# An adaLN attention and feed-forward block on one Trainium2 core: the gate's columns made earlier, a load of x made later, b2's rows behind b1's

## The chip, the core and the metric

The kernel runs on one core of a Trainium2 chip. The metric is the device time of one execution in microseconds; lower is better. In the profile, PE is TensorE (matmuls), PEld its weight loads, DVE VectorE, ACT ScalarE, POOL GpSimd and SP the engine that issues most of the DMAs. "SPq" and "ACTq" are the sequencers of SP and ACT when they issue a DMA.

## What is computed

There are 8 batches of 1024 rows of 256 numbers, all in f32. Each batch has six vectors of 256 that come from its condition `c`; two of them are gates, kept away from zero.

```
mod = (silu(c) @ wmod).reshape(8, 6, 1, 256)          # sa, ca, ga, sb, cb, gb
ga, gb = sign(g) * max(|g|, 0.25)                      # for both gates
h = layernorm(x) * (1 + ca) + sa
x = x + ga * softmax((h*w_lhs) @ (h*w_rhs).T) @ h
h = layernorm(x) * (1 + cb) + sb
x = x + gb * (relu(h @ W1 + b1) @ W2 + b2)             # W1 256x1024, W2 1024x256
```

## The kernel before

**Tiles and steps.** A batch is worked in eight steps of 128 rows (`i`, 0 to 7) and kept as two halves of 512 rows (`x_t[b, g]`). The main loop runs over batches and steps. Step `i` of batch `b` makes the scores of a row block two steps ahead (`direct`, matmuls at L433; steps 6 and 7 make those of the next batch's rows 0 and 1), takes their row maximum (`row_max`, L484), turns the maximum on PE (`max_turn`, L489), subtracts (`subtract`, L496), applies the exponent on ACT (`exponent`, L505) and multiplies by the normalized x (`product`, L522 and the paired forms). From batch 1 on, the feed-forward of the batch before is spread over the same steps: `pair_products` (L730, PSUM tiles pa, pb, pc), `pair_sums`, `pair_last`, `pair_relu`, and the second matrix (L810). Batch 0 has no feed-forward beside it.

**Mirrored scores.** The score matrix is symmetric up to the two weight vectors, so only blocks on and right of the diagonal are multiplied. `mirror(b, i)` fills the rest. In batch 0 it does so with transposes on PE. From batch 1 on, DVE turns 32 x 32 blocks (L456, tile Tm), four DMAs on SP write them to a scratch in DRAM (L327, `D_m<-Tm`), and a fifth reads them back in their new place (L330, `sc<-D_m`). The maximum of row `i` needs the mirrored blocks of all rows above it. The same five DMAs (`move`) turn the normalized x of the next batch (`D_a`; for batch 1 it is read back into `Y_early` and `X_early`, in steps 2 and 3 of batch 0, and used by `prepare_turn` in steps 5 and 6, which makes lT and rT, L386 and L396) and the input of the feed-forward (`D_f`, read back to X_f and used by `ffn_turn`, L709 and L711).

**What sets the order.** The order of the program's lines is kept on each engine (`pin`), so an instruction that waits holds all behind it on its engine; SP's DMAs are issued in order too. Loads of x for the next batches go out on ACT's queue (`load_x`, L86), into six buffers.

**The columns.** Four small row tiles are loaded at the start, turned on PE and copied by ACT into `cols` (`columns`, L178 and L179): `wv` holds w_lhs, w_rhs and b2 as six rows of 128, `b1_rows` holds b1 as eight. `w_cols(side)` picks two columns: side 0 is w_lhs, 1 is w_rhs, 2 is b2. `wv` is turned early in the start, `b1_rows` in `make_columns`, in step 0 of batch 0.

**The gate of the feed-forward.** `mod_direct` (L225) makes the feed-forward's vectors as columns, in the start. `make_gcol` makes the gate from them (four DVE instructions, L992 to L995), multiplies it by b2 (L1034), and stores for the last batch both results in DRAM (`last_d`, two DMAs at L1036 on SP, 256 numbers each, one by one since neighbours in a row of `gcol` are a batch apart). `gcol` is read from step 4 of batch 1 on (`y_gate`, L861, at 126.6 us) and `last_d` near the end (L899, at 696.2 us). `make_gcol` is called by `keep_columns`, in step 6 of batch 0, between the transpose of the scores of batch 1's row 0 and their maximum.

**The start.** SP issues in this order: c, x (second quarter of batch 0), w_lhs, w_rhs, b2, the last two quarters of x, the last two thirds of wmod (L119), b1 (L120), W1, W2 and the x of batch 1. ACT's queue takes the first quarter of x and the first third of wmod. PE waits at 12.07 us for wmod's later part (`mod_rows(2, 1)`, L198).

Of the kernel before, what the change touches and what calls it, by code (L numbers as in the profile page):

```python
# [13 lines left out]
ALU = mybir.AluOpType  # L14
# [3 lines left out]
P = 128  # L18
# [6 lines left out]
def adaln_block_kernel(  # L25
# [13 lines left out]
    nc = tc.nc  # L39
# [3 lines left out]
    ND = D // P  # L43
    NI = INTER // P
# [39 lines left out]
    def load_x(b, g, queue=nc.scalar):  # L84
        x_t[b, g] = two.tile([P, TH, D], F32, tag="x", name=f"x_{b}_{g}", bufs=6)
        queue.dma_start(  # L86
            out=x_t[b, g],
            in_=x[b, ts(g, HALF), :].rearrange("(t p) d -> p t d", p=P),
        )
# [3 lines left out]

    early_d = two.tile([P, 4, D], F32, tag="X", name="early_d", bufs=1)
    c_sb = early_d[:B, 0]
    wv, b1_rows = early_d[: 3 * ND, 2, 0:P], early_d[:NI, 3, 0:P]
    nc.sync.dma_start(out=c_sb, in_=c)
    for g in range(2):
        x_t[0, g] = two.tile([P, TH, D], F32, tag="x", name=f"x_0_{g}", bufs=6)
# [2 lines left out]
    def load_x0(q, queue):  # L102
        queue.dma_start(out=x_t[0, q // 2][:, ts(q % 2, 2), :], in_=x0_v[:, ts(q, 2), :])
# [9 lines left out]
    nc.sync.dma_start(  # L113
        out=wv[ND : 2 * ND, :], in_=w_rhs.rearrange("a b (k p) -> (a b k) p", p=P)
    )
    nc.sync.dma_start(out=wv[2 * ND : 3 * ND, :], in_=b2.rearrange("(k p) -> k p", p=P))
    load_x0(2, nc.sync)
    load_x0(3, nc.sync)
    nc.sync.dma_start(out=wm[:, :, 2 * D : 6 * D], in_=wmod_v[:, :, 2 * D : 6 * D])  # L119
    nc.sync.dma_start(out=b1_rows, in_=b1.rearrange("(k p) -> k p", p=P))  # L120
    w1 = const.tile([P, ND, INTER], F32, name="w1")
    w2 = const.tile([P, NI, D], F32, name="w2")
    nc.sync.dma_start(out=w1, in_=W1.rearrange("(k p) i -> p k i", p=P))
# [49 lines left out]
    cols = const.tile([P, NI + 3 * ND], F32, name="cols")  # L173

    def columns(src, at):
        n = src.shape[0]
        pv = ps_t.tile([P, HALF], F32, tag="t", name=f"pt_v{at}")
        nc.tensor.transpose(pv[:, :n], src, ident[:n, :n])  # L178
        nc.scalar.copy(cols[:, ds(at, n)], pv[:, :n])  # L179

    b1_col = lambda i: cols[:, i : i + 1]

    w_cols = lambda side: cols[:, ds(NI + side * ND, ND)].rearrange(
        "p (k b) -> p k b", b=1
    ).to_broadcast([P, ND, B])

# [6 lines left out]
    def mod_rows(part, parts):  # L193

        pm = ps_a.tile([P, HALF], F32, tag="a", name=f"pmr_{part}")
        w = parts * D
        for k in range(ND):
            nc.tensor.matmul(  # L198
                pm[:B, :w],
                lhsT=scT[:, k, :],  # L200
                rhs=wm[:, k, ds(part * D, w)],
                start=(k == 0),
                stop=(k == ND - 1),
            )
        nc.scalar.copy(
            mod[:, part : part + parts, :].rearrange("b s d -> b (s d)"), pm[:B, :w]
        )
# [73 lines left out]
    def prepare_stats(b, g, tiles=range(TH)):  # L281

        if tiles[0] == 0:
            mv = work.tile([P, TH, 2], F32, tag="mva", name=f"mva_{b}_{g}")
            pre[b, g] = [mv]
        mv = pre[b, g][0]
        for j in tiles:
            stats(mv, j, x_t[b, g][:, j, :], f"a{b}_{g}_{j}")

    def prepare_rstd(b, g):  # L290
        pre[b, g].append(rstd_of(pre[b, g][0], "ra", f"ra_{b}_{g}"))

    def prepare_norm(b, g, tiles=range(TH)):

        mv, r = pre[b, g]
        if b > 0:
            shift = work.tile([P, TH], F32, tag="rs", name=f"rs_{b}_{g}")
            nc.vector.scalar_tensor_tensor(shift, mv[:, :, 0], -1.0, r, ALU.mult, ALU.mult)
        for j in tiles:
            t = g * TH + j  # L300
            if b > 0:
                nc.scalar.activation(
                    xg_t[b][:, t, 0:D], x_tile(b, t), AF.Identity,
                    scale=r[:, j : j + 1], bias=shift[:, j : j + 1],
                )
                continue
            engine = nc.vector if j < TH // 2 else nc.gpsimd
            engine.tensor_scalar(
                xg_t[b][:, t, 0:D], x_tile(b, t), mv[:, j, 0:1], r[:, j : j + 1],
                ALU.subtract, ALU.mult,  # L310
            )
# [346 lines left out]
    def spare():  # L658
        if queue:
            queue.popleft()()  # L660
# [4 lines left out]
    def ffn_rstd(b, g):  # L665
        mv = mvb_t.pop((b, g))
        ffn["r", g] = mv, rstd_of(mv, "rb", f"rb_{b}_{g}")
# [15 lines left out]
    def x_plus(b, g):  # L683

        for t in range(g * TH, (g + 1) * TH):
            xr = x_tile(b, t)
            later(xr, xr, rows_t[b][:, 1, :], ALU.add)

    def xg_times(b, g):

        for t in range(g * TH, (g + 1) * TH):
            xg = xg_t[b][:, t, 0:D]
            later(xg, xg, rows_t[b][:, 0, :], ALU.mult)
# [256 lines left out]
    prepare_stats(0, 0, range(2, TH))  # L950
    prepare_rstd(0, 0)
    mod_rows(0, 2)
    columns(wv, NI)
    prepare_stats(0, 1, range(2))
    prepare_norm(0, 0)
    prepare_stats(0, 1, range(2, TH))
# [33 lines left out]
    def make_gate(out, raw, size, sign):  # L990

        nc.vector.tensor_scalar(sign, raw, 0.0, 2.0, ALU.is_ge, ALU.mult)  # L992
        nc.vector.scalar_tensor_tensor(size, raw, -1.0, raw, ALU.mult, ALU.max)
        nc.vector.tensor_scalar(size, size, GATE_MIN, None, ALU.max)
        nc.vector.scalar_tensor_tensor(out, sign, -1.0, size, ALU.add, ALU.mult)  # L995
# [33 lines left out]
    gcol = const.tile([P, 2, ND, B], F32, name="gcol")  # L1029
    last_d = dram.tile([2, D], F32, name="last_d")  # L1030

    def make_gcol():
        make_gate(gcol[:, 0], mod_ffn[:, 2], MB[:, 0], MB[:, 1])
        nc.vector.tensor_tensor(gcol[:, 1], gcol[:, 0], w_cols(2), ALU.mult)  # L1034
        for j in range(2):
            nc.sync.dma_start(  # L1036
                out=last_d[j].rearrange("(k p) -> p k", p=P), in_=gcol[:, j, :, B - 1]
            )
# [33 lines left out]
    def make_columns():  # L1072
        columns(b1_rows, 0)
        nc.gpsimd.tensor_tensor(b1_step, cols[:, NH:NI], cols[:, 0:NH], ALU.subtract)

    def keep_columns():
        nc.vector.tensor_copy(modT[:, 0], mod_ffn[:, 0])
        nc.vector.tensor_scalar(modT[:, 1], mod_ffn[:, 1], 1.0, None, ALU.add)
        make_gcol()

    def early(b, i):

        if b == 0:

            if i in (1, 2):
                prepare_rstd(1, i - 1)
            elif i == 4:
                ffn_rstd(0, 0)
            if i in (1, 2):
                prepare_norm(1, i - 1)  # L1090
                x_plus(1, i - 1)
            if i in (3, 4):
                xg_times(1, i - 3)
            elif i == 5:
                prepare_turn(1, 0)
                ffn_norm(0, 0)
            elif i == 6:
                load_x(2, 0)
        else:
            if i == 2 and b + 1 < B:  # L1100
                prepare_norm(b + 1, 0)
            elif i == 6 and b + 2 < B:
                load_x(b + 2, 0)
# [24 lines left out]
    def norms(b, i):  # L1128
        if b > 0 and i == 0:
            ffn_blocks(b - 1, 1)  # L1130
        if b == 0:
            if i == 0:
                prepare_start(1)
        elif b + 1 < B:
            if i == 1:
                prepare_start(b + 1)
                prepare_stats(b + 1, 0)
            elif i == 2:
                prepare_blocks(b + 1, 0)
                x_plus(b + 1, 0)  # L1140
                xg_times(b + 1, 0)
        elif i == 5:

            ffn_blocks(b, 0)
        if b == B - 1:
            return
        if i == 6 and b > 0:
            ffn_blocks(b, 0)
# [7 lines left out]
    for b in range(B):  # L1156
        for i in range(NT):
# [27 lines left out]
            if b == 0:  # L1185
                if ahead[0] == 0:
                    row_max(*ahead)
                else:
                    mirror(*ahead)
                turns(b, i)  # L1190
                product(b, i, (0,))
                spare()
                if i in (0, 1):
                    prepare_stats(1, i)
                if ahead[0] == 0:
                    mirror(*ahead)
                if last_exponent:
                    exponent(*last_exponent)
                last_exponent = ahead if ahead[0] == 0 else None
                early(b, i)  # L1200
                spare()
                product(b, i, (1,))
                if ahead[0] == 0:
                    max_turn(*ahead)
                product_out(b, i)
                spare()
                if ahead[0] == 0:
                    subtract(*ahead)
                if i == 0:
                    make_columns()  # L1210
                norms(b, i)
                spare()
                if i == NT - 1:
                    assert not queue
                    right_sums(1, range(4))
                continue
# [243 lines left out]
```

## Time and profile before

| | us |
|---|---|
| median of 3 runs | 768.96 |
| lowest and highest run | 765.62, 770.04 |
| the profiled execution | 765.82 |
| its span, first to last instruction | 764.0 |
| PE busy in it | 750.9 |
| busy DVE, POOL, ACT | 572.2, 571.0, 376.4 |

The span's mean granted TensorE clock is 0.998 of full speed. The times in the views count from the span's start; the profiled execution takes 1.82 us more than its span. "Idle before" and the arrow behind an instruction name what its engine waited for last.

Where things stand in time around the change: step 1 of batch 0 ends on PE at 38.8 us, step 6 runs from 58.1 and step 7 from 68.0; batch 1 begins at 71.7.

### The profile page before, as it was taken

How to read it: one execution, taken by the hardware profiler on the slowest of the kernel's cores; microseconds unless marked ns; L12 is line 12 of the kernel's file. 1: busy time of each engine (PE TensorE's matmuls, PEld its weight loads, DVE VectorE, ACT ScalarE, POOL GpSimd, SP SyncE). 2: the span in 40 equal slices, each digit the busy share in tenths (PEclk: the TensorE clock that was granted, in tenths of full speed). 3: DMA queues.
4: the chain of work that ended last, by engine and by line, in shares of the span. 5: the costliest groups of instructions: out<-in, count | busy, mean ns of one | idle time of the engine just before them, and what ended most of it. 6: DMA issues, size and time to landing. Idle time of an engine off the chain costs nothing.

```text
span 764.0 us, 11903 instructions
## 1 busy us (share of the span) xinstructions
PE 750.9 (98%) x3876; PEld 625.1 (82%) x3876; DVE 572.2 (75%) x1261; ACT 376.4 (49%) x690; POOL 571.0 (75%) x658
## 2 busy tenths in 40 slices
PE   8999799999999999999999999999999999999998
PEld 3786588888898888978888888888889788888887
DVE  6786588868787786968779688886879677685632
ACT  3465444644466353754537454464546635243521
POOL 3761677679978789687886889777996788669731
PEclk9999999999999999999999999999999999999999
DMA  8033743355534554435534455335552454133220
GB/s 302 17 112 112 104 137 98 116 154 157 153 96 124 169 170 125 113 120 164 152 107 145 127 154 159 95 115 154 159 165 66 130 167 140 50 89 127 79 88 28
DMA packets 107466, 96.24 MB, mean 126 GB/s; under 512 B 30318, under 2 KB 99972, under 8 KB 107404
## 3 DMA queue, kind: packets, MB, share of 16 engines
q1 hardware_dynamic: 99660, 86.84, 39.7%
q10 hardware_dynamic: 7744, 8.65, 3.6%
q8 instruction: 30, 0.49, 0.3%
q14 instruction: 32, 0.26, 0.1%
HBM read 51.13 MB, written 44.32 MB: 125 GB/s over the span
## 4 chain that ended last, share of the span: by engine, by line
PE 90%; DMA 4%; DVE 3%; ACT 1%; issue 1%; SPq 1%; DVEq 0%
PE psc L433 16%; PE pa L730 10%; PE po L522 9%; PE pr L614 7%; PE pb L730 6%; PE yc L810 6%; PE pc L730 6%; PE ya L810 6%; PE yb L810 6%; PE pq L614 5%; PE pp L570 5%; PE py L920 4%; PE yd L810 3%; DMA D_m<-Tm 1%; DMA wm<-in_L_wmod_dram 1%; PE pm L489 1%
## 5 line engine op out<-in xcount | busy, mean ns | idle before, releaser
L433 PE MATMUL psc<-rT,lT 128*128 128x512 f32 (+3 forms) x384 | 135.0, 487 | 0.5 <-ACT rT L363 0.5
L784 POOL TENSOR_TENSOR f<-f,kept 128x512 f32<-128x512 f32 x64 | 81.5, 1274 | 49.7 <-DVE f L783 23.0
L505 ACT ACTIVATE pT<-pT 128x1024 f32<-128x1024 f32 x64 | 67.6, 1056 | 75.4 <-DVE pT L496 75.3
L440 ACT COPY sc<-psc 128x512 f32<-128x512 f32 (+3 forms) x96 | 44.8, 475 | 114.4 <-PE psc L433 106.2
L496 DVE TENSOR_TENSOR pT<-sc,pm 128x1024 f32<-128x1024 f32 x64 | 77.3, 1208 | 30.2 <-PE pm L489 14.9
L433 PEld LDWEIGHTS psc<-rT,lT 128*128 128x128 f32 x384 | 66.4, 191 | 38.0 <-issue 25.5
L484 DVE TENSOR_REDUCE m<-sc 128x1 f32<-128x1024 f32 x64 | 77.4, 1209 | 11.2 <-DMA sc<-D_m 9.1
L522 PE MATMUL po<-xg,pT 128*128 128x257 f32 x352 | 80.7, 380 | 0.5 <-DVE rs_f L675 0.5
L522 PEld LDWEIGHTS po<-xg,pT 128*128 128x128 f32 x352 | 66.2, 190 | 11.3 <-issue 1.2
L751 ACT COPY kept<-pa 128x512 f32<-128x512 f32 x64 | 37.4, 584 | 71.2 <-PE pa L730 71.2
L730 PE MATMUL pb<-hs,w1s 128*128 128x256 f32 x256 | 66.7, 383 | 1.8 <-DVE f L769 1.1
L730 PE MATMUL pc<-hT,w 128*128 128x256 f32 x256 | 65.7, 379 | 0.0
L884 POOL TENSOR_TENSOR x<-x,Y 128x512 f32<-128x512 f32 x28 | 35.1, 1277 | 30.8 <-DMA Y<-D_y 25.4
L730 PEld LDWEIGHTS pb<-hs,w1s 128*128 128x128 f32 x256 | 49.0, 192 | 9.7 <-DVE f L769 2.0
L793 ACT ACTIVATE f<-f 128x512 f32<-128x512 f32 x64 | 39.8, 623 | 33.8 <-POOL f L784 33.7
L663 POOL TENSOR_TENSOR x<-x,rows 128x256 f32<-128x256 f32 x64 | 44.8, 732 | 13.7 <-ACT rows L1025 10.5
L730 PEld LDWEIGHTS pc<-hT,w 128*128 128x128 f32 x256 | 48.7, 190 | 6.7
L810 PE MATMUL yc<-f,w2s 128*128 128x256 f32 x224 | 51.3, 379 | 0.0
L456 DVE STREAM_TRANSPOSE Tm<-sc 128x896 f32<-128x896 f32 (+6 forms) x49 | 34.3, 700 | 19.0 <-ACT sc L440 17.0
L810 PEld LDWEIGHTS yc<-f,w2s 128*128 128x128 f32 x224 | 41.5, 190 | 8.1 <-issue 2.9
L570 PEld LDWEIGHTS pp<-xg,pT 128*128 128x128 f32 x336 | 41.9, 192 | 5.1 <-issue 1.4
L803 POOL TENSOR_TENSOR ft<-f 128x256 f32<-128x256 f32 x56 | 40.8, 729 | 6.5 <-ACT f L794 6.5
(164 smaller groups left out, 1820.1 us busy)
## 6 DMA issues: line engine op xcount, KB each, us to landing
D_f<-T_f SPq DMA_DIRECT2D x64, 128.0 KB, 2.4
X_f<-D_f SPq DMA_DIRECT2D x16, 512.0 KB, 3.5
D_a<-T_a SPq DMA_DIRECT2D x56, 128.0 KB, 2.3
D_y<-T_y SPq DMA_DIRECT2D x56, 128.0 KB, 2.7
Y<-D_y SPq DMA_DIRECT2D x14, 512.0 KB, 4.7
out_dram<-x SPq DMA_DIRECT2D x14, 512.0 KB, 4.4
x<-in_L_attn_x_dram ACTq DMA_DIRECT2D x12, 512.0 KB, 3.3
X_a<-D_a SPq DMA_DIRECT2D x12, 512.0 KB, 3.5
```

The lines of the kernel that those rows point to most:

```text
L433: nc.tensor.matmul(psc[:, : hi - lo], lhsT=lT_t[b, i // TH][:, k, ts(i % TH, P)], rhs=rT_t[b, n][:, k, lo - n * HALF : HALF], start=(k == ...
L440: nc.scalar.copy(score_row(b, i)[:, lo // V : hi // V, :], psc[:, : hi - lo].rearrange("p (n v) -> p n v", v=V),)
L484: nc.vector.tensor_reduce(m, score_row(b, i), AX.XY, ALU.max)
L496: nc.vector.tensor_tensor(pT.rearrange("p j (a v) -> p j a v", v=V), score_columns(b, i), pm[:, :P].rearrange("p (j a v) -> p j a v", j=1, ...
L505: nc.scalar.activation(pT_t[b, i], pT_t[b, i], AF.Exp)
L522: nc.tensor.matmul(po[:, : D + 1], lhsT=pT[:, t, :], rhs=xg_t[b][:, t, 0 : D + 1], start=(t == 0), stop=(t == NT - 1),)
L570: nc.tensor.matmul(out, lhsT=lhs[:, t, :], rhs=xg_t[b][:, h * TH + t, P : P + XS], start=(t == 0), stop=(t == TH - 1),)
L614: nc.tensor.matmul(out, lhsT=lhs[:, t, :], rhs=rhs[:, t, :], start=(t == 0), stop=(t == TH - 1),)
L663: queue.append(lambda: nc.gpsimd.tensor_tensor(out, in0, row, op))
L730: nc.tensor.matmul(out, lhsT=lhsT, rhs=rhs, start=True, stop=True)
L784: nc.gpsimd.tensor_tensor(f[:, c::NH, hi], f[:, c::NH, hi], kept[:, None, hi].to_broadcast([P, 2, H2]), ALU.add,)
L810: nc.tensor.matmul(out, lhsT=lhs(c), rhs=rhs(c), start=(c == 0), stop=(c == NH - 1))
```

## The change

`make_gcol` moves from `keep_columns` (step 6 of batch 0) to step 1 of batch 0, behind that step's `subtract`, with its five DVE instructions and its two stores. The load of the first half of x of batch 2 moves from step 6 to step 7 of batch 0; there it stands on ACT behind the second instruction of `ffn_turn`. The load of b2 moves on SP from the third of the small row loads to behind b1, and its rows are turned together with b1's in `make_columns` instead of with w_lhs and w_rhs; so `wv` has four rows in place of six, `b1_rows` ten in place of eight, and the order of `cols` is b1, b2, w_lhs, w_rhs. `make_gcol` can so not stand ahead of `make_columns` (step 0).

```diff
-    wv, b1_rows = early_d[: 3 * ND, 2, 0:P], early_d[:NI, 3, 0:P]
+    wv, b1_rows = early_d[: 2 * ND, 2, 0:P], early_d[: NI + ND, 3, 0:P]
...
-    nc.sync.dma_start(out=wv[2 * ND : 3 * ND, :], in_=b2.rearrange("(k p) -> k p", p=P))
     load_x0(2, nc.sync)
     load_x0(3, nc.sync)
     nc.sync.dma_start(out=wm[:, :, 2 * D : 6 * D], in_=wmod_v[:, :, 2 * D : 6 * D])
-    nc.sync.dma_start(out=b1_rows, in_=b1.rearrange("(k p) -> k p", p=P))
+    nc.sync.dma_start(out=b1_rows[0:NI], in_=b1.rearrange("(k p) -> k p", p=P))
+    nc.sync.dma_start(out=b1_rows[NI:], in_=b2.rearrange("(k p) -> k p", p=P))
...
-    w_cols = lambda side: cols[:, ds(NI + side * ND, ND)].rearrange(
+    w_cols = lambda side: cols[:, ds(NI + ND + side * ND, ND)].rearrange(
...
-    columns(wv, NI)
+    columns(wv, NI + ND)
...
     def make_gcol():
         make_gate(gcol[:, 0], mod_ffn[:, 2], MB[:, 0], MB[:, 1])
-        nc.vector.tensor_tensor(gcol[:, 1], gcol[:, 0], w_cols(2), ALU.mult)
+        nc.vector.tensor_tensor(gcol[:, 1], gcol[:, 0], w_cols(-1), ALU.mult)
         for j in range(2):
             nc.sync.dma_start(
                 out=last_d[j].rearrange("(k p) -> p k", p=P), in_=gcol[:, j, :, B - 1]
             )
...
     def keep_columns():
         nc.vector.tensor_copy(modT[:, 0], mod_ffn[:, 0])
         nc.vector.tensor_scalar(modT[:, 1], mod_ffn[:, 1], 1.0, None, ALU.add)
-        make_gcol()
...
-            elif i == 6:
+            elif i == 7:
                 load_x(2, 0)
...
                 if i == 0:
                     make_columns()
+                elif i == 1:
+                    make_gcol()
                 norms(b, i)
```

## The prediction, made before the result was known

> **What bounds the kernel now.** I read the page's busy shares, then the waits of the PE (TensorE) queue, then busy time by stretch, and then the chain and the order of time for the one stretch that stands out.
>
> ```profile
> PE 750.9 (98%) x3876; PEld 625.1 (82%) x3876; DVE 572.2 (75%) x1261; ACT 376.4 (49%) x690; POOL 571.0 (75%) x658
> ```
>
> The waits (engine and line, what it waited for: us in all, times, longest):
>
> ```profile
> PE pa L730 <- ACT kept L751: 3.0, 1, 3.0
> ...
> PE pb L730 <- DVE f L769: 1.1, 1, 1.1
> PE pm L489 <- DVE m L484: 0.6, 1, 0.6
> PE pb L730 <- POOL hs L720: 0.6, 1, 0.6
> ```
>
> PE is busy 98% of 764.0 us, so some 13 us are open in all, and the few waits above are nearly all of what is open in mid-kernel. They lie in one place (columns: stretch, its length, busy PE, PEld, DVE, ACT, POOL, granted clock, DMA share, GB/s):
>
> ```profile
> 60.00:74.00 14.00, 14.00 (x49) 8.99 (x48) 9.48 (x23) 6.65 (x12) 0.47 (x1) 1.00 0.49 145
> 74.00:100.00 26.00, 20.21 (x80) 15.22 (x79) 16.24 (x33) 10.65 (x21) 16.75 (x19) 0.93 0.67 104
> 100.00:190.00 90.00, 89.97 (x478) 75.79 (x477) 71.83 (x158) 47.23 (x87) 73.28 (x84) 1.00 0.45 132
> ```
>
> From 74 to 100 us, where batch 0 hands over to batch 1, PE is open for 5.79 us and its granted clock falls to 0.93; behind it PE is full for 90 us, and so it is to about 590. What PE gains at 100 us therefore reaches the end. The chain through that stretch (start, length):
>
> ```profile
> 75.03 0.60 SPq L1036
> ...
> 77.65 9.17 DMA D_m<-Tm
> ...
> 86.90 4.08 DMA sc<-D_m
> ...
> 95.62 2.64 PE pa L730 x6
> ```
>
> D_m, the mirrored scores of row 1 of batch 1, needs 9.17 us to land; its kind (96 KB) has a median of 3.3. Ahead of it on SP's queue stand the two `last_d` stores of L1036. After it comes everything in order: the read back to sc, row 2's maximum on DVE at 91.00, the subtraction of row 1 at 92.14, the exponent on ACT, behind which `kept` waits in ACT's order, and PE's pa at 95.62. The DMA view of 76 to 78 us shows what the stores are:
>
> ```profile
> DMA packets 1170, 0.53 MB, mean 264 GB/s; under 512 B 565, under 2 KB 1170, under 8 KB 1170
> ```
>
> Two stores of 1 KB with 4 bytes at a time make 512 of these 565 small packets. From 80 to 85 us next to nothing moves (3 to 7 GB/s; 8 packets from 80 to 82) though D_m has not landed; at about 85.6 its packets go on. I read this as D_m held by the stores until 10.6 us after their first issue.
>
> Before that, X_f of batch 0 is late, beside the 512 KB load of x for batch 2:
>
> ```profile
> 65.24 0.38 ACTq L86 DMA_DIRECT2D x<-in_L_attn_x_dram  x1
> ...
> 72.90 0.55 DVE L709 TENSOR_SCALAR hT<-X_f,modT 128x512 f32<-128x512 f32 x1 [3.01 <-DMA X_f<-D_f]
> ...
> 77.95 1.22 DVE L484 TENSOR_REDUCE m<-sc 128x1 f32<-128x1024 f32 x1 [3.15 <-DMA sc<-D_m]
> ```
>
> **The change, part by part.** *make_gcol leaves keep_columns.* Five DVE instructions of 0.17 us (67.00 to 67.87, 0.87 us together) and the stores' 1.12 us of issue leave step 6 of batch 0. On DVE nothing follows: the next two, a maximum of 1.21 and the transpose at 68.92, wait there for a score copy that ends at 68.82. On SP the stores leave the way of D_m(1,1). Without them I let it land in 3.3 us. Its issue starts right behind the read of sc(1,0): in before 74.37, so landing would be near 80, the read's 4.08 gives 84, and DVE, which has finished L783 at 85.09, would go straight on to row 2's maximum instead of at 91.00. Then the subtraction, the exponent and `kept` are done before PE asks. What goes: PE's open time from 90 to 96 (0.33 + 1.68 + 1.62 = 3.63 us by stretches of 2 us), and the clock. Behind the 3.02 us wait the granted clock reads 0.50 at 96:98 and 0.66 at 98:100: six pa need 2.64 us (1.30 at 127.95, at full clock), four pb 1.47 (0.86). That is 1.34 + 0.61 = 1.95 us. Together **5.58 us**.
>
> The Trainium skill, "TensorE: Matmul & The Clock Gate" (Part 1), lets the clock fall to half after about one idle window of 3.4 us and says that this window runs free; the row (3.02 us open, then 0.50) fits, and by that rule the 1.95 us would differ from run to run, so that the sum below would be anything from 4.8 to 6.7 us.
>
> *x of batch 2 a step later.* In step 7, ACT issues the load behind L711, which waits for X_f, so at about 71 to 72 instead of 65.24. X_f then shares the engines no longer. A quiet D_f lands 1.85 us behind its last issue (719.69 to 721.54; here 65.19 to 67.48, 2.29), X_a needs 3.5 (here 67.48 to 72.86, 5.4): X_f is there up to 2.3 us earlier, at 70.6. The wait of pb for POOL's hs (0.56) goes. D_m(1,0), 4.6 us from last issue to the read in before, lands at 72 to 73 and its read to sc starts 1.4 to 2.5 us earlier. But there the x load now lies: 512 KB at 357 or 264 GB/s (stretches 6:7 and 76:78) are 1.5 to 2.0 us, of which I charge 0.8 to 1.3 to that read. Sc(1,0) is in place 0.6 to 1.9 us earlier, and so are the chain of DVE behind it (77.95), the pb wait of 1.13 us and the exponent that product(1,0) waits for at 83.21 (0.47 us). Ends 0.6 and 1.9 us with the delay of the next part in them; I take **1.2**, the middle. The later load costs nothing by itself: its statistics are first read at 102.94.
>
> *make_gcol arrives in step 1.* DVE takes its 0.87 us behind L496 (ends 41.79). The row maxima that follow end 0.4, 0.4 and 0.1 us before PE turns them (44.33, 49.42, 53.97), and DVE's open times at 44.37 (0.3 us) and 53.36 (0.8) take the rest: nothing, at most 0.3. The stores go out at 42.7 on an empty queue, and behind them on SP stands the following (start, issue time, engine, line):
>
> ```profile
> 44.40 1.79 SPq L327 DMA_DIRECT2D D_a<-T_a  x4
> 48.14 0.34 SPq L330 DMA_DIRECT2D Y_early<-D_a  x1
> 49.81 2.83 SPq L327 DMA_DIRECT2D D_a<-T_a  x4
> 54.57 0.34 SPq L330 DMA_DIRECT2D X_early<-D_a  x1
> ```
>
> D_a is what they can hold now. From below, nothing: Y_early is read at 48.9, later only by DVE's delay. From above, as D_m was held: it landed 11.8 us after the first store's issue, so the read is at 54.5. I take 54.0, near the upper end, as that row is the only one of these stores; the sc read that stood ahead of them in before is missing. Then Y_early lands at 57.5 (3.5 as X_a), in time for 57.72. The second D_a (1.95 to issue, as at 165.65, and 2.6 to land) lets X_early be read at 58.9, in place at 62.4. ACT's two rT (1.50) end at 63.9; PE asks at 63.3 for the second half of direct(1,0). So PE loses 0.6 us, already in the 0.6 to 1.9 above; every us beyond a read at 53.4 costs one. The Trainium skill, "DMA: Bandwidth & Descriptors" (Queues, rings and completion order), says that a completion signal lands only after every earlier write of that DMA engine. By this D_a inherits the stores' whole delay; that is the upper end, and speaks against the change.
>
> *b2 behind b1.* One issue of 0.25 us leaves SP ahead of load_x0(2), and one of 0.30 arrives behind wmod, ahead of W1, which starts at 6.03 with a wait for the first wmod half and is needed at 28.79. wmod's second half, for which PE waits 1.20 us at 12.07, is issued at 4.12 and may go out 0.3 to 0.6 earlier. But the DMA share is 1.0 from 3 to 16 us, all loads ahead of it stay ahead, and so I book nothing (0 to 0.6 gained). The column copies keep their count; 6 become 4 columns, 8 become 10.
>
> **Sum.** 5.58 + 1.2 = 6.8, less 0.1 for DVE: 6.7 us. The profiled execution took 765.82 (span 764.0 and 1.8 around it): 759.1. It is one of the fast ones of runs from 765.62 to 770.04; 6.7 off their median is 762.3. Outside this stretch PE waits for nothing over 0.5 us between 100 and 700, so part of the spread may lie in it; the profile can't say. I take **760.5**, between the two, and 757 to 764.5 as this case's own range.
>
> **Rivals.**
> *The late sc(1,1) stays late* (0.15): what held D_m was not the stores, or the x load, now queued ahead of it, takes their place. For it: the load is 512 KB at just that time. Against it: the other six D_m of this size land in 3.3, and DMA is nearly idle from 80 to 85. The 5.58 us stay and 1.1 go: 764.7, by the median 767.9.
> *D_a held too long* (0.06), slower: the stores hold D_a longer than they held D_m, as 512 packets of D_a join them. Each us after 53.4 delays X_early, rT and direct(1,0); from 3 us of wait on, the clock adds its 1.95. It outweighs the gain from a read at about 59, and with a read at 64 (21 us after the stores' issue) the time is 759.1 + 10 + 1.95 = 771. For it: 9.17 us was already far from 3.3. Against it: those packets were gone 10.6 us after issue with a busier queue.
> *The start gains too* (0.07): wmod's second half lands earlier by what SP waits less, PE's 1.20 us go: 758, by the median 761.
> *The forecast* (0.72).
>
> A measurement can tell 0.5%, 3.8 us, from no change: faster is under 765.1. The forecast and the start's gain are faster, 0.79; the late sc is within, 0.15; the held D_a is slower, 0.06. To leave out no more than 2 in 10 the range runs from 756.5 to 767.9, the late sc included.
>
> **What would show it.** Right: D_m(1,1) lands in 3 to 4 us; the granted clock is 1.00 from 74 to 100; no 3.0 us wait of pa for `kept`; the read of Y_early moves from 48.14 to about 54; an rT wait of some 0.6 us at 63. Wrong: Y_early still read at 49 (the stores are cheap on an empty queue: step priced too high), a D_m behind the x load that still lands after 9 us, or a wait over 3 us at 61 to 66.

## The result and the profile after

The changed kernel takes 763.43 us (median of 12 runs, 760.78 to 766.28) against 767.43 us (12 runs, 764.06 to 770.04): 4.0 us less, ratio 0.9949 with a 95% interval of 0.9928 to 0.9970. The forecast was 760.5 us, a gain of 6.7. It had the direction, and the place where time is won; in the profile, more than half of what is won there is given back elsewhere. The profiled execution took 764.15 us, span 762.4; it is to be compared with the 765.82 of before with care, since the 12 executions of either kernel spread over 5 us and more, and only one of each has a trace.

First the stretches, with the same columns as in the prediction:

```profile
44.00:60.00 16.00, 15.61 (x75) 12.69 (x74) 14.57 (x27) 8.86 (x18) 8.57 (x13) 1.00 0.38 54
60.00:74.00 14.00, 11.71 (x34) 6.71 (x33) 9.16 (x21) 7.54 (x13) 0.00 (x0) 0.88 0.44 138
74.00:100.00 26.00, 25.53 (x115) 20.27 (x114) 19.19 (x38) 12.76 (x23) 17.26 (x19) 1.00 0.56 170
```

From 74 to 100 us PE is open for 0.47 us where it was 5.79, at a clock of 1.00 where it was 0.93: the stall of the hand-over is gone. But from 60 to 74, where PE had been full, it is now open for 2.29 us and the clock is 0.88. SP's own rows say why (start, length of the issue):

```profile
44.55 0.88 SPq L1036 DMA_DIRECT2D last_d<-gcol  x2
47.09 8.93 SPq L327 DMA_DIRECT2D D_a<-T_a  x4
57.78 0.34 SPq L330 DMA_DIRECT2D Y_early<-D_a  x1
58.22 1.91 SPq L327 DMA_DIRECT2D D_a<-T_a  x4
63.18 0.34 SPq L330 DMA_DIRECT2D X_early<-D_a  x1
...
78.21 2.14 SPq L327 DMA_DIRECT2D D_m<-Tm  x4
83.50 0.52 SPq L330 DMA_DIRECT2D sc<-D_m  x1
```

The lower two rows are the forecast's gain: D_m(1,1) is read back 3.15 us behind its last issue, no longer 8.8. The upper five are the price: D_a stands behind the two stores now. Its four issues, 1.79 us in before, take 8.93, its read waits until 57.78, and X_early's read moves from 54.57 to 63.18. That ends on PE (two rows of the changed kernel, in order of time):

```profile
66.42 1.52 ACT L396 ACTIVATE rT<-X_early,sides 128x512 f32<-128x512 f32 x2 [1.25 <-DMA X_early<-D_a]
...
68.00 6.68 PE L433 MATMUL psc<-rT,lT 128*128 128x512 f32 x12 [2.29 <-ACT rT L396]
```

ACT makes rT only when X_early is there, and PE stands still for 2.29 us. The clock then reads 0.84, 0.50 and 0.80 in the three stretches of 2 us from 68. The same twelve matmuls of the scores (PSUM tile psc), behind the same wait but at a clock of 1.00, need 4.99 us in the run with make_gcol alone (below):

```profile
66.59 4.99 PE L433 MATMUL psc<-rT,lT 128*128 128x512 f32 x12 [1.89 <-ACT rT L396]
```

One ledger for the two profiled executions, in us of PE's time:

| place | lost before | lost after | won |
|---|---|---|---|
| start, to the first matmul of L225 (begins at 25.42, after at 25.16) | | | 0.3 |
| fall of the clock at 28 us (see the last section) | 0 | 1.7 | -1.7 |
| 44 to 74 us | 0 | 0.39 and 2.29 open, 1.7 by the clock (6.68 less 4.99) | -4.4 |
| hand-over, 74 to 100 us | 5.79 open, 1.95 by the clock | 0.47 open | 7.3 |

Together 1.5 us are won by this count; the spans differ by 1.6.

### The profile page after: what moved, and what is told of

It is laid out like the page before. It is cut to its first block, busy times and chain, and to the rows that moved or that the text cites. A ratio compares the mean times of both kernels' runs of the same rounds, so it can differ in the third digit from the quotient of the medians.

```text
span 762.4 us, 11902 instructions
## 1 busy us (share of the span) xinstructions
PE 752.6 (99%) x3876; PEld 625.8 (82%) x3876; DVE 574.5 (75%) x1261; ACT 376.5 (49%) x690; POOL 570.9 (75%) x658
## 4 chain that ended last, share of the span: by engine, by line
PE 92%; DVE 3%; DMA 2%; ACT 1%; SPq 1%; issue 1%; DVEq 0%; ACTq 0%
PE psc L433 15%; PE pa L730 10%; PE pr L614 7%; PE po L522 7%; PE pc L730 7%; PE pb L730 7%; PE yc L810 6%; PE ya L810 6%; PE yb L810 6%; PE pq L614 5%; PE pp L570 5%; PE py L920 4%; PE yd L810 3%; PE pm L489 1%; SPq L327 1%; DMA D_a<-T_a 1%
## 5 line engine op out<-in xcount | busy, mean ns | idle before, releaser
L433 PE MATMUL psc<-rT,lT 128*128 128x512 f32 (+3 forms) x384 | 136.9, 492 | 2.9 <-ACT rT L396 2.9
L522 PE MATMUL po<-xg,pT 128*128 128x257 f32 x352 | 81.9, 384 | 0.5 <-DVE rs_f L675 0.5
L522 PEld LDWEIGHTS po<-xg,pT 128*128 128x128 f32 x352 | 67.0, 192 | 11.5 <-issue 1.2
L751 ACT COPY kept<-pa 128x512 f32<-128x512 f32 x64 | 37.4, 584 | 69.4 <-PE pa L730 67.2
L718 POOL TENSOR_TENSOR hs<-hT 128x256 f32<-128x256 f32 x16 | 11.6, 726 | 46.1 <-DVE hT L709 46.1
L570 PEld LDWEIGHTS pp<-xg,pT 128*128 128x128 f32 x336 | 41.9, 192 | 5.1 <-DVE st_b L262 1.4
```

Source lines behind the costliest of these rows:

```text
L433: nc.tensor.matmul(psc[:, : hi - lo], lhsT=lT_t[b, i // TH][:, k, ts(i % TH, P)], rhs=rT_t[b, n][:, k, lo - n * HALF : HALF], start=(k == ...
L522: nc.tensor.matmul(po[:, : D + 1], lhsT=pT[:, t, :], rhs=xg_t[b][:, t, 0 : D + 1], start=(t == 0), stop=(t == NT - 1),)
L570: nc.tensor.matmul(out, lhsT=lhs[:, t, :], rhs=xg_t[b][:, h * TH + t, P : P + XS], start=(t == 0), stop=(t == TH - 1),)
```

## The experiments

The theory after the result: the two stores of 4-byte pieces hold all DMA work queued behind them for some 12 us, wherever they stand; the change moved the hold from D_m to D_a and made it cheaper, not free. (The hold is counted here from the first store's issue to the read of the DMAs queued behind it.) The first rival: the gain comes from the x load.

**The three parts alone.** Each is the kernel before with one part of the diff.

> One part alone: make_gcol with its two stores in step 1; the x load stays in step 6, b2 stays where it was. Theory (the two stores of 4-byte pieces hold whatever DMA writes are queued behind them for some 10 us; the change moved that hold from D_m to D_a): D_m(1,1) lands in 3 to 4 us, the 3.0 us wait of pa for kept and the half clock at 96 to 100 are gone, the read of Y_early moves from 48 to about 54 to 58, an rT wait of 1 to 2.5 us appears at 61 to 68; 2 to 4 us faster than before. Rival (the gain comes from the x load leaving the way of D_f, X_f and D_m): within 1 us of before, the D_m beside the x load still late.

> One part alone: the x load of batch 2 in step 7; the stores stay in step 6, in front of D_m(1,1). Theory: D_m(1,1) still takes 9 us or more to land and the wait for kept with its half clock stays; X_f lands 1 to 2 us earlier; 0 to 1.5 us faster than before. Rival (the x load was the cause): 3 to 4 us faster, D_m(1,1) lands in under 5 us.

> One part alone: b2's rows behind b1's. Theory: wmod's second half is issued about 0.5 us earlier and lands a few tenths earlier; within 0.5 us of before. Rival (the half clock seen near 28 us in the changed kernel comes from the earlier start): the granted clock falls at 28 to 32 here too, and the time is 1 to 2 us longer than before.

The edits are lines of the diff above, in the second only this one:

```diff
-            elif i == 6:
+            elif i == 7:
                 load_x(2, 0)
```

| | median us | ratio to before | 95% interval |
|---|---|---|---|
| before, of these runs (31) | 766.21 | | |
| make_gcol alone (12) | 764.71 | 0.9991 | 0.9967 to 1.0014 |
| x load alone (12) | 762.87 | 0.9962 | 0.9941 to 0.9983 |
| b2 alone (12) | 765.59 | 0.9998 | 0.9975 to 1.0021 |

The ratio is not the quotient of the two medians beside it: for make_gcol alone that would be 0.9980, which lies in the interval. The three ratios multiplied make 0.9951, the whole 0.9949. How they divide was not expected: make_gcol alone gains 0.7 us by its ratio (the interval goes from 2.5 gained to 1.1 lost), where 2 to 4 were expected, as its rival had it. Its trace is as the theory had it: D_m(1,1) is read 2.4 us behind its last issue, the hold has moved as in the changed kernel, and the rT wait is 1.9 us:

```profile
43.53 0.88 SPq L1036 DMA_DIRECT2D last_d<-gcol  x2
46.08 7.68 SPq L327 DMA_DIRECT2D D_a<-T_a  x4
56.49 0.34 SPq L330 DMA_DIRECT2D Y_early<-D_a  x1
```

The time from the turn of b1's rows in step 0 (L178) to the first matmul of L570 in batch 1 (tile pp) spans the places that the change touches and leaves out the start and the fall of the clock at 28. It is 68.5 us in before, 65.3 here and 67.2 with the x load alone. So the traces give make_gcol 3.2 us and the load 1.3, and the times give 0.7 and 2.9. The profiled execution with make_gcol alone is one of the fastest of its 12 (763.18 us, clock 1.000), and their mean clock is 0.9964 against 0.9957 in before; where the others lose what the trace wins, no run shows.

With the x load alone D_m stays as late as before (issue at 75.88, read at 86.29), and the wait for `kept` stays. (This trace is of the slowest of the 12, 766.67 us.)

```profile
PE pa L730 <- ACT kept L751: 2.9, 1, 2.9
```

```profile
75.88 1.92 SPq L327 DMA_DIRECT2D D_m<-Tm  x4
86.29 0.52 SPq L330 DMA_DIRECT2D sc<-D_m  x1
```

So the rival is wrong on D_m's cause, which is not the load, but in the time it is nearer than the theory's 0 to 1.5 us: the part measures 2.9 (0.38%, interval 1.3 to 4.5). What it removes is there in the trace: PE is open for 3.73 us from 74 to 100 instead of 5.79, as the waits of pb and of the maximum shrink. The rest goes with the clock. The mean granted clock of its 12 runs is 0.9981, that of the 31 runs of before 0.9957; over the latter, time rises by 0.85 us for each 0.001 of clock (a straight line through the 31 points, 762.6 us at 1.000), so by that line 2.0 of the 2.9 go with the clock. That fewer open microseconds let the clock fall less often is my reading of this; it is not shown by itself.

The trace of b2 alone has a half clock at 28 to 32 us (0.71 and 0.50 in its two stretches), as its rival said. The 12 runs show no loss, and their interval, from 1.9 us gained to 1.6 lost, leaves little of the rival's 1 to 2 us.

**The stores as rows.** The same 512 numbers, turned by one transpose on PE and stored as four rows of 512 bytes, in the changed kernel and in the kernel before. The three dots stand for lines that name the tiles. `store_last` is called in step 2 in the changed kernel, between the two moves of D_a, and in step 7 in the kernel before, behind D_m(1,1); so the store changes its form and its place on SP.

```diff
-        for j in range(2):
-            nc.sync.dma_start(
-                out=last_d[j].rearrange("(k p) -> p k", p=P), in_=gcol[:, j, :, B - 1]
-            )
+    def store_last():
+        ...
+        last = gcol.rearrange("p j k b -> p (j k) b")[:, :, B - 1]
+        nc.tensor.transpose(pl[:n, :P], last, ident)
+        nc.scalar.copy(last_rows[:n, :], pl[:n, :P])
+        nc.sync.dma_start(
+            out=last_d.rearrange("j (k p) -> (j k) p", p=P), in_=last_rows[:n, :]
+        )
```

> The changed kernel with the same numbers stored as four rows of 512 bytes (one transpose on PE, one copy on ACT, one store in step 2) in place of 512 pieces of 4 bytes. Theory: no hold anywhere; D_a is read back 2 to 3 us behind its last issue, no rT wait at 61 to 68, no late D_m; 3.5 to 5 us faster than the changed kernel, 7 to 9 faster than before. Rival (D_a is late for another reason, such as x, the loads or the order on SP): the rT wait stays, the time is that of the changed kernel within 1 us.

> The kernel before with the 512 pieces of 4 bytes replaced by four rows of 512 bytes, stored in step 7 behind the mirror's DMAs; the gate stays in step 6, the x load too. Theory (the stores alone made D_m late): D_m(1,1) is read back 2 to 3 us behind its last issue and not 9 to 10, no 3.0 us wait of pa for kept; the waits of pb and the late X_f beside the x load stay; 3 to 5 us faster than before. Rival (it takes the x load's move as well): within 1.5 us of before.

> The changed kernel with the rows stored as in the run with four rows of 512 bytes, but the x load back in step 6. Theory: X_f lands 1 to 2 us later than with the load in step 7 and the waits of pb for hs and f (0.6 and 1.1 us) come back: 1 to 2 us slower than that run, some 761. Rival (once the stores are gone the load may stand anywhere): within 0.5 us of it, 759.7.

| | median us | before beside it | ratio | 95% interval |
|---|---|---|---|---|
| changed kernel, rows (8) | 759.65 | 766.21 | 0.9915 | 0.9881 to 0.9949 |
| kernel before, rows (6) | 761.32 | 766.98 | 0.9930 | 0.9906 to 0.9954 |
| changed kernel, rows, x load in step 6 (6) | 762.09 | 766.98 | 0.9939 | 0.9916 to 0.9962 |

In the changed kernel the rows take the rT wait away (no such row is left among PE's waits), and D_a is read 1.96 us behind its last issue:

```profile
44.80 1.78 SPq L327 DMA_DIRECT2D D_a<-T_a  x4
48.54 0.34 SPq L330 DMA_DIRECT2D Y_early<-D_a  x1
```

In the kernel before, with gate and x load where they were, D_m is read back 2.3 us behind its last issue; from 74 to 100 us PE is open for 2.51 us in place of 5.79, at a clock of 1.00:

```profile
75.41 2.11 SPq L327 DMA_DIRECT2D D_m<-Tm  x4
79.83 0.52 SPq L330 DMA_DIRECT2D sc<-D_m  x1
80.40 0.52 SPq L1043 DMA_DIRECT2D last_d<-last_rows  x1
```

That rows hold nothing where they do stand ahead is seen at the second D_a of the changed kernel with rows: the store goes out at 48.97, D_a is issued from 49.93 on for 2.17 us, and X_early is read at 55.12, 3.0 us behind the last issue. In the changed kernel, where no store stands between the two moves, that is 3.05 us (58.22, 1.91 and 63.18).

All waits went as the theory said; the gains are 6.6 us where it had 7 to 9, 5.7 where it had 3 to 5, and the load in step 6 costs 2.4 by the medians where it had 1 to 2. The first two rivals are out. The third, that the load may stand anywhere, is out by the waits of pb, which are back (1.5 and 0.5 us); the two times alone would not decide it. The store as rows, with gate and load left where they were, gains 0.7%, against 0.5% for the whole change (the intervals overlap). From the turn of b1's rows to the first pp of batch 1, the changed kernel needs 65.6 us, with rows 62.4, and the kernel before with rows 63.1, against 68.5 in before. So the hold on D_a costs 3.2 us, and without it the stretch gains 6.1 us, close to the 6.7 of the forecast. By time, the changed kernel with rows and without them are not told apart clearly (0.9881 to 0.9949, and 0.9928 to 0.9970).

**Another place, another queue.** The same stores in step 0, and the stores of step 1 on ACT's queue:

```diff
                 if i == 0:
                     make_columns()
-                elif i == 1:
                     make_gcol()
```

```diff
-            nc.sync.dma_start(
+            nc.scalar.dma_start(
                 out=last_d[j].rearrange("(k p) -> p k", p=P), in_=gcol[:, j, :, B - 1]
             )
```

> The changed kernel with make_gcol in step 0, right behind make_columns: the same stores of 4 bytes, issued near 36 us in place of 44.5, with no DMA behind them before 45. Theory (a hold of 12 to 13 us from the first issue): they are gone by 48 to 49, so D_a is read back near 49 to 50, no rT wait; 1.5 to 4 us faster than the changed kernel, 760 to 762. Rival (D_a is late in the changed kernel for another reason): the read of Y_early stays at 56 or later.

> The changed kernel with the two stores issued on ACT's queue in place of SP's. Theory A (the hold is in each DMA engine, whichever queue the pieces came by): the read of Y_early is late as before, 55 to 58, and the rT wait stays; the time is that of the changed kernel within 1 us or up to 1 us longer, for ACT's issue time. Theory B (the hold is in SP's own queue, in order): D_a is read back at 48 to 50, no rT wait; 2 to 4 us faster than the changed kernel.

Step 0: 761.10 us, ratio 0.9928 (0.9906 to 0.9950), as expected. The stores went out at 39.05 and not at 36, and the read of Y_early comes at 52.11 and not near 49 to 50, 13.1 us behind the first store. D_a's four issues are at 1.78 again, its read is 0.7 us later behind them than with rows, and 0.6 us of an rT wait is left:

```profile
39.05 0.88 SPq L1036 DMA_DIRECT2D last_d<-gcol  x2
47.68 1.78 SPq L327 DMA_DIRECT2D D_a<-T_a  x4
52.11 0.34 SPq L330 DMA_DIRECT2D Y_early<-D_a  x1
```

On ACT's queue: 763.22 us, ratio 0.9949 (0.9928 to 0.9970), the time of the changed kernel. D_a, on SP, is held all the same, from 46.69 to 54.90, 12.2 us behind the first store:

```profile
42.68 0.89 ACTq L1036 DMA_DIRECT2D last_d<-gcol  x2
...
44.25 0.90 PE L473 MATMUL ptm<-ident,sc 128*128 128x128 f32 x3 [2.26 <-ACT sc L440]
...
46.69 1.77 SPq L327 DMA_DIRECT2D D_a<-T_a  x4
54.90 0.34 SPq L330 DMA_DIRECT2D Y_early<-D_a  x1
```

So the hold is not SP's order of issue; it lies behind the two queues, in what they share: the DMA engines or the memory that they write, which these runs don't tell apart. (The Trainium skill speaks for the engines, "DMA: Bandwidth & Descriptors", Queues, rings and completion order: a completion lands only after every earlier write of that engine, across its queues.) SP's issue is not blocked here: the four take 1.77 us. The rT wait, which was expected to stay, is 0.6 us. In its place ACT waits for the gate and PE for ACT, 2.26 us at 44.25, and the clock behind that reads 0.52 and 0.62 from 44 to 48.

**What in the stores is slow.** Three kernels with rows for `last_d`, and beside them, in step 1 on SP, stores of 4-byte pieces into a scratch that nothing reads: one store of 256 adjacent pieces, in the form of `last_d`'s own, and both stores with 512 bytes from piece to piece (the diff) or with 64 (16 in place of P in the scratch's shape).

```diff
+    spare_d = dram.tile([2, D, P], F32, name="spare_d")
...
+        for j in range(2):
+            nc.sync.dma_start(
+                out=spare_d[j, :, 0].rearrange("(k p) -> p k", p=P),
+                in_=gcol[:, j, :, B - 1],
+            )
```

> A dose: the kernel with four rows of 512 bytes, and in step 1 on SP one further store of 256 pieces of 4 bytes into a scratch nothing reads (half of the 512). Theory (each piece costs the engines a fixed time): half the hold, the read of Y_early at 49 to 52. Rival (a fixed wait for any such store): at 55 to 58 as with both.

> The kernel with four rows of 512 bytes, and in step 1 on SP two further stores of 256 pieces of 4 bytes each into a scratch nothing reads, with 512 bytes from one piece to the next. Theory C (the pieces are slow because neighbours share memory lines): little hold, the read of Y_early at 48 to 50. Theory D (each 4-byte write costs the same wherever it goes): at 55 to 58.

> As the run with the pieces 512 bytes apart, but 64 bytes apart: two further stores of 256 pieces of 4 bytes into a scratch nothing reads. Theory E (a write holds only others within the same 64 bytes): no hold, the read of Y_early at 48 to 50. Theory F (the shared unit is larger, up to 512 bytes): a hold between none and that of adjacent pieces, the read at 50 to 58, with 8 pieces in 512 bytes where adjacent ones have 128.

Half the pieces, adjacent:

```profile
44.53 0.36 SPq L1036 DMA_DIRECT2D spare_d<-gcol  x1
47.08 1.78 SPq L327 DMA_DIRECT2D D_a<-T_a  x4
56.89 0.34 SPq L330 DMA_DIRECT2D Y_early<-D_a  x1
```

All pieces, 512 bytes apart:

```profile
42.06 0.88 SPq L1037 DMA_DIRECT2D spare_d<-gcol  x2
44.62 1.78 SPq L327 DMA_DIRECT2D D_a<-T_a  x4
48.29 0.34 SPq L330 DMA_DIRECT2D Y_early<-D_a  x1
```

All pieces, 64 bytes apart:

```profile
44.00 0.88 SPq L1037 DMA_DIRECT2D spare_d<-gcol  x2
46.55 1.78 SPq L327 DMA_DIRECT2D D_a<-T_a  x4
50.28 0.34 SPq L330 DMA_DIRECT2D Y_early<-D_a  x1
```

The dose went against the theory and with its rival, a fixed wait: 256 adjacent pieces hold D_a until 12.4 us after their issue, 512 until 13.2 in the changed kernel. But 512 pieces with 64 or 512 bytes from one to the next hold nothing: D_a is read 1.9 us behind its last issue, though queue, place and size of the pieces are those of the changed kernel. (One run each: 763.12, 760.06 and 761.73 us.) It is therefore neither the number of small writes nor their size. What is left is that they are neighbours. The small packets themselves are recorded as fast in both forms, 544 from 42 to 46 us with 64 bytes and with make_gcol alone; only in the latter D_a then crawls (48 and 35 GB/s in the two stretches of 4 us from 46, against 135 and 177). A distance between 4 and 64 bytes was not tried. Why neighbours are slow, and why one store costs almost as much as two, no run here shows.

**One step further.** With rows, the longest wait left in the hand-over is pb's for DVE (0.7 us), behind the read of sc(1,0), which the x load meets in step 7. So the load went to the end of step 0 of batch 1.

```diff
             if i == 0 and b + 1 < B:
                 load_rows(b + 1)
+                if b == 1:
+                    load_x(2, 0)
```

> The changed kernel with four rows of 512 bytes and the x load of batch 2 once more later, at the end of step 0 of batch 1. Theory (in step 7 the load shares the engines with the read of sc(1,0), for which DVE and then pb wait): sc(1,0) lands about 1 us earlier, the 0.7 us wait of pb for DVE goes, 758.5 to 759.7 and so 0.9 to 1.1% faster than before. Rival (the load now meets the DMAs of rows 1 and 2, or batch 2's statistics): as fast as with the load in step 7 or up to 1 us slower.

It takes 760.36 us against 768.01 of before beside it, ratio 0.9892 (0.9866 to 0.9918). The ratio is in the expected range, the median 0.7 us above it, and pb's wait, which was to go, is 0.5 us. It beats both kernels clearly, since the changed kernel's interval (0.9928 to 0.9970) lies above. It can't be told from the version with the load in step 7 (0.9881 to 0.9949).

## Why the prediction was right, and where it was not

- **The number**: the forecast of 760.5 lies 2.9 us below the median. The range, 756.5 to 767.9, holds the median of before (767.43) too, so that the time lies in it says little; the waits in the traces say more.
- **What bounds the kernel**: right. PE is full outside the start and the hand-over, and what is won there reaches the end.
- **D_m is held by the stores**: right, and shown in the kernel before with rows, where nothing but the store was changed and D_m is read back after 2.3 us. The 5.58 us for the wait and the clock behind it went in the trace: there the stretch to pp is 5.4 us shorter. By time the split of the sum did not come out: with 5.58 less 0.6 for rT and 0.1 for DVE, make_gcol alone should have won 4.9 us, and it measured 0.7. That the forecast of the whole came nearer is so in part luck: the load measured more than its 1.2. The 1.95 us of clock are not in every execution either: one of the 31 runs of before stands at a clock of 1.000.
- **The x load, 1.2 us**: right in kind, and in the trace (1.3 us). By itself it measures 2.9 us (1.3 to 4.5), most of it with the clock. The working behind the 1.2 does not hold: a read that starts 1.4 to 2.5 us earlier, less 0.8 to 1.3 for the load, is 0.1 to 1.7 us, and not 0.6 to 1.9. With the rows the load in step 7 is 0.24% faster than in step 6 by the two ratios (1.8 us; 2.4 by the medians, which stand beside different runs of before), and the two intervals overlap.
- **make_gcol in step 1, the term that failed.** The prediction let D_a be read at 54.0 and charged 0.6 us for rT. It was read at 57.78, and the rT wait measured 2.29 us in the changed kernel and 1.9 alone, with 1.7 us of clock behind the former. Two sizes were off. The stores went out at 44.55 and not at 42.7: 1.4 us of this is PE's own delay (1.7 lost at the fall of the clock at 28, 0.3 won in the start), the rest DVE, where L992 and L994 took 0.47 and 0.59 us in place of 0.17. The hold lasted 13.2 us from the first issue where I had 11.8 from D_m as the upper end and took less. The five DVE instructions in step 1, charged with 0.1 us, come with 0.39 us of open PE from 44 to 60 (0.36 with rows, none in before). The rule given for the price, one us for each us after 53.4, holds: 57.78 less the 2.1 by which PE itself was late is 2.3 us past it. So the rival "D_a held too long" came true in small, within the forecast. The prediction named the sentence on completions of the Trainium skill ("DMA: Bandwidth & Descriptors", Queues, rings and completion order) as what speaks against the change; D_a did inherit the whole delay, and the prediction should have taken the upper end and beyond.
- **b2 behind b1, nothing**: right, 0.9998 (0.9975 to 1.0021).
- **The start**: the rival's 1.2 us did not come as a gain of the change; b2 alone shows nothing.
- **The clock** was booked once, behind the wait for `kept`. In the runs it goes with the largest part of the spread between executions: of the 31 runs of before 14 stand at a mean clock of 0.996 (median 766.4 us), 8 at 0.998 (764.1) and one at 1.000 (762.1).

## What to carry to other kernels

When a slow transfer is moved off one path, ask what stands behind it in its new place: here stores that took 12 to 13 us held what was queued behind them for that long, on SP and across the two queues tried, so such a store belongs where nothing is issued for that long, or has to be made fast. Look at the form of a store before its place: here four rows in place of 512 neighbouring words of 4 bytes gained at least as much as moving three things. And price an unseen wait from the one row that shows the same operation, without a discount for a quieter surrounding.

## What the runs showed that was not expected

- 256 adjacent 4-byte writes to DRAM hold the DMAs behind them for about 12 us; 512 of them 64 bytes apart hold nothing that shows (what is behind them is read back after 1.9 us). With adjacent pieces the hold is nearly the same wherever they stand: 11.9 us in before, 13.0 and 13.2 in step 1, 13.1 in step 0, 12.2 on ACT's queue.
- A held DMA need not show at its issuer: four issues took 8.93 and 7.68 us in the changed kernel and with make_gcol alone, but 1.83 in before, 1.77 with the stores on ACT's queue and 1.78 with half the pieces, where the read was late all the same.
- The clock falls without any open time on PE as well. In the changed kernel PE is busy without a gap from 20 to 34 us, and the clock is 0.60 and 0.54 in the two stretches from 28 to 32, behind 24 matmuls of 8 columns (L225); eight matmuls of the product (L522, po) then need 2.97 us, not 1.74. Of the 14 traces here, including those of before and after, six show this fall (after, b2 alone, step 0, half the pieces, 64 bytes apart, x load in batch 1), all with b2's rows moved, as four of the others have, and none of the four without. Those 24 matmuls stand in every one of the traces. Whether the earlier start has a part in it stays open; the times of b2 alone show no loss. The Trainium skill, "TensorE: Matmul & The Clock Gate" (Part 1), ties the fall to an idle window of about 3.4 us; here 2.29 us of wait were followed by one, and 2.26 with the stores on ACT's queue, 1.9 us with make_gcol alone were not, and this one had none.
- A small DVE instruction seems to wait for POOL. In the run with make_gcol in step 0, L994 and L995 (16 elements each) took 1.23 and 1.19 us and ended at 37.80 and 39.02, where POOL's operations L982 and L983 ended at 37.77 and 39.00; with POOL idle, in the kernel before, they took 0.17 and 0.18. The stores of that run went out 2 us later for it. That the ends meet is all that the trace shows.
